# A planner's load and power times, its distance ahead of TensorE, and the last batch's end in pieces

## The chip, the core and the metric

The kernel runs on one core of a Trainium2 chip. The metric is the time of one execution on the device in microseconds. Three runs of the kernel before took 1474.4, 1475.67 and 1474.44 us; the median is 1474.44.

## What is computed

There are 16 batches of 1024 nodes with 128 features, and one adjacency matrix of 1024 x 1024 zeros and ones.

```
h   = x @ others_weight
e   = leaky_relu(pairs of u1 + u2);  att = softmax over nodes of where(adj > 0, e, -9e15)
x   = layernorm(x + att @ h + x @ self_weight)             # layer 0, a graph attention
h   = x                                                    # layer 1, a gated graph network
5 times:
    m = adj @ h
    z = sigmoid([m, m] @ w3.T + h @ u3.T + b);  r = sigmoid([m, m] @ w4.T + h @ u3.T + b)
    v = tanh([m, m] @ w5.T + (r * h) @ u5.T + b)
    h = (1 - z) * h + z * v
x   = layernorm(x + h)
```

## The kernel before

Everything is float32. The products with the adjacency matrix are made exact in two passes: `split` (L590 to 602) rounds a block to fp32r on ACT and takes the rest on DVE, and `product` (L605 to 615) sends both parts through TensorE, eight matmuls of 512 columns for a half of a batch. The gate products have float32 operands. Each batch is kept transposed (features on partitions, 1024 nodes in two halves of 512 columns) in a tile `hT`.

Batches go in pairs `q`, each with five steps `s`. For most pairs and steps, `messages` computes m of both batches together from seven products instead of eight quarters (tiles `blk_x11` to `blk_s4`, banks `ps_acc_a`, `ps_acc_c`, `gz`); for the pairs and steps in `PLAIN` each batch has its own products (`ps_acc<-adj,blk_h`). `gates` follows: a product with u3 (`pu`, L1159), a copy of its bank for z on ACT (L1162), two gate products (L1169), two tanh on ACT (L1172), r*h on DVE (L1179), two products into the bank v (L1185, L1186), tanh on ACT (`hv`, L1189) and three DVE operations that make the new h (L1196, L1203, L1210).

`leave` sends h on. As a rule the half is turned on DVE in 32x32 blocks (`turn`, L566), stored to DRAM by four DMAs (`away`, L576, X<-T) and loaded by one (`back`, L584, G<-X), which completes the transposition. Where `on_pe` says so, TensorE transposes it instead (L558) and `split` reads the bank. After the last step, `leave` loads the kept input of layer 1 (`o<-yd`, L1253), adds h (L1261), and calls `layernorm`: statistics on DVE (L527, L529), four small GpSimd instructions that make the factor and the offset (L533, L534, then L536 and L537 or, for the other sign, L539 and L540), four scales on ACT (L545), and a store (L1272). Layer 0 ends in the same `layernorm`, from `F_y` tiles that came through DRAM.

The order of the work is planned when the program is built. Every operation is added to a `Plan` with an engine, a length in nanoseconds, a rank, and the values it reads and writes. `order` plays the plan: an engine that is free takes the ready operation of the lowest rank for which tiles are free; a successor becomes ready after the length and a lag, which depends on the engine or is given with the operation. The sequence in which operations start is the program's order on every engine. On the chip each engine then takes its instructions in that order and waits for what each needs, so the planned times themselves leave no trace but the order.

The rank of a step is `10 * (b // 2) + 4.2 * s` plus an offset from the table `D` (L300). Lengths that matter here: GpSimd's part of `layernorm` 2200, the lag of `back` 2300. `IDLE` (80) and `HUM` (60) operations of two transposes of the identity each, of rank 9000, are taken by TensorE where the plan has nothing else for it; hum becomes ready only with the last pair's step 3. `o` and `y0` have two buffers each.

Of the kernel before, what the change touches and what calls it, by code (L numbers as in the profile page):

```python
# [12 lines left out]
AF = mybir.ActivationFunctionType  # L13
# [3 lines left out]
P = 128  # L17
# [8 lines left out]
LOW, HIGH = -20.0, 100.0  # L26
TINY = 1e-30
PLAIN = {(0, 0), (0, 1), (0, 2), (7, 2), (7, 3), (7, 4)}
LATER = 2.5
AHEAD = range(4, 12)  # L30
TURNED = {(0, 0), (7, 3)}
IDLE = 80
HUM = 60


class Plan:
# [36 lines left out]
    def order(self):  # L73
        ops, free = self.ops, dict(self.slots)
        users, left = [[] for _ in ops], []
        uses = {}
        for i, (_, _, _, _, deps, tiles) in enumerate(ops):
            left.append(len(deps))
            for d in deps:
                users[d].append(i)  # L80
            for t in tiles:
                uses[t] = uses.get(t, 0) + 1
        ready, busy, live = {}, {}, set()
        at = {}
        events = [(0, 0, i) for i in range(len(ops)) if not left[i]]
        heapq.heapify(events)
        started = []
        while events:
            now = events[0][0]
            while events and events[0][0] == now:  # L90
                _, what, i = heapq.heappop(events)
                engine, _, rank, _, _, tiles = ops[i]
                if what == 0:
                    heapq.heappush(ready.setdefault(engine, []), (rank, i))
                elif what == 1:
                    busy.pop(engine)
                    for t in tiles:
                        uses[t] -= 1
                        if not uses[t]:
                            free[t[0]] += 1  # L100
            more = True
            while more:
                more = False
                for engine, queue in ready.items():
                    if engine in busy:
                        continue
                    later = []
                    while queue:
# [26 lines left out]
def kernel(  # L135
# [79 lines left out]
    def exact(pools):  # L215
# [210 lines left out]
        def hum_():  # L426
            for j in range(2):
                nc.tensor.transpose(T(("ps", "hum"))[:, j * P : (j + 1) * P], ident, ident)

        def hum():  # L430
            for i in range(HUM):
                pe(2 * TR, 9000, hum_, reads=[(("m", B - 1, STEPS - 2, 1), 0)], writes=[(("ps", "hum"), 0)])

        for i in range(IDLE):
            pe(2 * TR, 9000, idle_, reads=[(("ident",), 0)], writes=[(("ps", "idle"), 0)])

# [82 lines left out]
            dve(2 * V, 1 + c / 4, t24, reads=[*y, (("tab",), c, 0)], writes=[(("tab",), c, 1)])  # L519


        def layernorm(key, g, rank, after, src, dst, write, sg=1):
            stats, mv, rstd = ("stats", *key, g), ("mv", *key, g), ("rstd", *key, g)

            def look():
# [5 lines left out]
            def power():  # L531
                mean, var, r = T(mv)[:, :, 0], T(mv)[:, :, 1], T(rstd)
                nc.gpsimd.tensor_scalar(r[:, 0, :], var, EPS, None, ALU.add)  # L533
                nc.gpsimd.tensor_tensor(r[:, 0, :], r[:, 0, :], mhalf[:, 0:4], ALU.pow)  # L534
                if sg > 0:
                    nc.gpsimd.tensor_scalar(r[:, 1, :], mean, -1.0, None, ALU.mult)  # L536
                    nc.gpsimd.tensor_tensor(r[:, 1, :], r[:, 1, :], r[:, 0, :], ALU.mult)  # L537
                else:
# [10 lines left out]
            dve(1100, rank, look, reads=[after], writes=[(stats, 0), (mv, 0)])  # L549
# [3 lines left out]
        def transposes(src, read, t, rank):  # L553


            def emit():
                for j in range(4):
                    nc.tensor.transpose(T(t)[:, j * P : (j + 1) * P], src()[:, j * P : (j + 1) * P], ident)  # L558

            pe(4 * TR, rank, emit, reads=[*read, (("ident",), 0)], writes=[(t, 0)])  # L560

        def turn(t, src, read, rank):

# [16 lines left out]
        def back(d, t, rank, also=(), then=()):  # L580
# [440 lines left out]
        def messages(q, s, k):  # L1021
# [118 lines left out]
            combine(m[one, 1], c, ALU.add)  # L1140
            return [[(m[one, 0], 0), (m[one, 1], "part")], [(m[two, 1], "part")] * 2]

        def gates(b, s, soon):
            rank = rank_of(b, s)
            hT = ("hT", b)
# [3 lines left out]
            for e in range(2):  # L1149
# [35 lines left out]
                    nc.tensor.matmul(T(pv), wm[:, 2, :], T(m), start=True, stop=False)  # L1185
                    nc.tensor.matmul(T(pv), u5h, T(r), start=False, stop=True)  # L1186

                def hv_(pv=pv, hv=hv):
                    nc.scalar.activation(T(hv), T(pv), AF.Tanh, bias=b5 if sg > 0 else nb5, scale=1.0)  # L1189

                pe(2 * F, rank + D["pv"], pv_, reads=[(m, 0), (r, 2), (("wm",), 0), (("uw",), 0)], writes=[(pv, 0)])
                act(A, rank + D["hv"], hv_, reads=[(pv, 0), (("wm",), 0)], writes=[(hv, 0)])
                dve(
                    V,
                    rank + D["h"],
                    lambda hv=hv, h=h: nc.vector.tensor_tensor(T(hv), T(hv), h(), ALU.subtract),  # L1196
                    reads=[(hv, 0), (hT, e)],
                    writes=[(hv, 1)],
                )
                dve(  # L1200
                    V,
                    rank + D["h"],
                    lambda hv=hv, z=z: nc.vector.scalar_tensor_tensor(T(hv), T(z), 1.0, T(hv), ALU.add, ALU.mult),  # L1203
                    reads=[(hv, 1), (z, 1)],
                    writes=[(hv, 2)],
                )
                dve(
                    V,
                    rank + D["h"],
                    lambda hv=hv, h=h: nc.vector.scalar_tensor_tensor(h(), T(hv), 0.5, h(), ALU.mult, ALU.add),  # L1210
                    reads=[(hv, 2)],
                    writes=[(hT, e)],
                )

        def leave(b, s):

# [2 lines left out]
            for g in range(2):  # L1219
# [18 lines left out]
                    continue  # L1238

                t = ("ps", "t", b, s, g)  # L1240
                if on_pe(b, s):
                    transposes(h, [(hT, g)], t, rank + D["tr"])
# [7 lines left out]
                sp(  # L1250
                    450,
                    rank + D["o"],
                    lambda o=o, yd=yd: nc.sync.dma_start(T(o).rearrange("p c d -> p (c d)"), T(yd)),  # L1253
                    reads=[(yd, 0), (hT, g)],
                    writes=[(o, "y")],
                )

                def last(t=t, o=o, flat=on_pe(b, s)):
                    x = T(o).rearrange("p c (a j) -> p c a j", a=4)
                    n = T(t).rearrange("p (c a j) -> p c a j", c=4, a=4) if flat else chunks(T(t))  # L1260
                    nc.vector.tensor_tensor(x, n, x, ALU.add)  # L1261

                dve(V, rank + D["o"], last, reads=[(t, 0), (o, "y")], writes=[(o, "raw")])

                def at(j, o=o):
                    return T(o)[:, j, :]

                layernorm(("o", b), g, rank + D["ln"], (o, "raw"), at, at, (o, 0), sign(b))
                sp(
                    450,  # L1270
                    rank + D["out"],
# [345 lines left out]
```

## Time and profile before

| | |
|---|---|
| median of three runs | 1474.44 us |
| the profiled execution | 1486.99 us, its span 1485.2 |
| mean granted TensorE clock | 0.995 of full speed |
| busy: TensorE, DVE, ACT, GpSimd | 1460.4, 1167.5, 900.1, 189.7 us |
| products with the adjacency (L608) | 2800 matmuls, 1.87 us for eight |
| gate products (L1159, L1169, L1185, L1186) | 0.86 us for the two passes of one |
| G<-X loads | 148 of 256 KB |
| X<-T stores | 584 of 64 KB |
| GpSimd's first instruction of a power (L533, y) | 227 to 3516 ns, median 505 |

The profile is of one execution, 12.6 us longer than the median. "Busy" of TensorE counts from a matmul's issue to its modelled end, and successive matmuls overlap, so a sum of busy times is more than the time they took; the chain of work that ended last shows what each adds. In the timeline a row has its start, its length, engine, source line, and in brackets the idle time before it and what ended that. A wait for several things is put down to the last. In the windows, each engine's busy time and number of instructions come first, then the granted clock, the share of the DMA engines, and what they moved.

### The profile page before, as it was taken

Reading aid. Unit: us, or ns where it says so; the run is one execution under the profiler, and the core shown is the slowest. Engines: PE = TensorE matmul, PEld = TensorE weight load, DVE = VectorE, ACT = ScalarE, POOL = GpSimd, SP = SyncE. Lnnn points to the kernel's source line nnn. Section 1 sums busy time; section 2 is a strip of 40 time slices with the busy share of each in tenths; the row PEclk is TensorE's granted clock in tenths of the full one; section 3 lists DMA queues with packets and bytes.
Section 4 is the critical chain, followed back from the end, with each engine's and each line's share of the span. In section 5 each row is a group of like instructions: output and inputs, shape, how many; then the busy total and the mean of one; then the engine's idle time right before and its main releaser. Section 6 shows DMA issues by size and latency. Waiting matters only on the chain.

```text
span 1485.2 us, 18097 instructions
## 1 busy us (share of the span) xinstructions
PE 1460.4 (98%) x5148; PEld 915.9 (62%) x5148; DVE 1167.5 (79%) x2761; ACT 900.1 (61%) x1800; POOL 189.7 (13%) x265
## 2 busy tenths in 40 slices
PE   9999999999999999999999999999999999999998
PEld 7666655666565666665656566565666556556666
DVE  6778688889788698988888798876888877776534
ACT  5565565666566676656756666565665666654544
POOL 0111100112111020111300121210201202000102
PEclk9999999999999999999999999999999999999999
DMA  8325724465254653445435542445433454223301
GB/s 310 135 58 167 209 68 131 125 195 162 60 145 113 196 138 87 144 146 148 116 112 139 171 135 67 133 126 152 119 96 96 138 149 113 62 71 88 107 0 45
DMA packets 210113, 184.71 MB, mean 124 GB/s; under 512 B 35071, under 2 KB 156630, under 8 KB 210006
## 3 DMA queue, kind: packets, MB, share of 16 engines
q1 hardware_dynamic: 209442, 182.64, 42.9%
q8 instruction: 42, 0.69, 0.2%
q10 hardware_dynamic: 564, 0.85, 0.2%
q14 instruction: 65, 0.53, 0.1%
HBM read 101.97 MB, written 81.44 MB: 123 GB/s over the span
## 4 chain that ended last, share of the span: by engine, by line
PE 71%; DVE 8%; DMA 7%; POOL 5%; ACT 4%; issue 2%; SPq 2%; DVEq 0%; POOLq 0%; ACTq 0%
PE ps_acc_a L608 12%; PE ps_g_r L1169 7%; PE ps_g_v L1186 7%; PE gz L1169 7%; PE ps_g_v L1185 7%; PE ps_g_r L1159 7%; PE ps_acc_c L608 7%; PE ps_acc_po L608 5%; PE ps_acc L608 4%; PE gz L608 3%; DMA G<-X 3%; SPq L576 2%; POOL rstd_y L533 2%; ACT y L545 1%; PE ps_idle L416 1%
## 5 line engine op out<-in xcount | busy, mean ns | idle before, releaser
L1196 DVE TENSOR_TENSOR hv<-hv,hT 128x512 f32<-128x512 f32 x160 | 109.8, 686 | 90.1 <-ACT hv L1189 89.4
L1169 PE MATMUL ps_g_r<-m,wm 128*128 128x512 f32 x320 | 161.3, 603 | 8.7 <-ACT gz L1162 8.7
L1186 PE MATMUL ps_g_v<-r,u5h 128*128 128x512 f32 x320 | 163.5, 592 | 0.7 <-DVE r L1179 0.7
L1185 PE MATMUL ps_g_v<-m,wm 128*128 128x512 f32 x320 | 163.6, 592 | 0.0
L1169 PE MATMUL gz<-m,wm 128*128 128x512 f32 x320 | 159.4, 595 | 0.0
L1159 PE MATMUL ps_g_r<-hT,u 128*128 128x512 f32 x320 | 154.5, 595 | 0.0
L608 PE MATMUL ps_acc_a<-tab,blk_s 128*128 128x512 f32 x544 | 147.0, 412 | 5.4 <-ACT m L1112 5.3
L608 PE MATMUL ps_acc_po<-adj,blk 128*128 128x512 f32 x512 | 140.2, 420 | 0.0
L1172 ACT ACTIVATE r<-ps_g_r,bh 128x512 f32<-128x512 f32 x160 | 109.6, 687 | 43.6 <-PE ps_g_r L1169 43.3
L1172 ACT ACTIVATE z<-gz,bh 128x512 f32<-128x512 f32 x160 | 109.0, 687 | 31.3 <-PE gz L1169 31.2
L608 PEld LDWEIGHTS ps_acc_a<-tab,blk_s 128*128 128x128 f32 x544 | 101.3, 188 | 39.8 <-ACT m L1112 8.6
L1179 DVE SCALAR_TENSOR_TENSOR r<-r,hT 128x512 f32<-128x512 f32 x160 | 108.6, 684 | 20.7 <-ACT r L1172 20.5
L533 POOL TENSOR_SCALAR rstd_y<-mv_y 128x4 f32<-128x4 f32 x32 | 30.5, 954 | 738.5 <-DVE mv_y L529 671.6
L608 PEld LDWEIGHTS ps_acc_po<-adj,blk 128*128 128x128 f32 x512 | 95.9, 188 | 35.5 <-issue 10.8
L1162 ACT COPY gz<-ps_g_r 128x512 f32<-128x512 f32 x160 | 91.3, 573 | 32.0 <-PE ps_g_r L1159 29.7
L1210 DVE SCALAR_TENSOR_TENSOR hT<-hv,hT 128x512 f32<-128x512 f32 x160 | 108.8, 680 | 1.8
L1203 DVE SCALAR_TENSOR_TENSOR hv<-z,hv 128x512 f32<-128x512 f32 x160 | 108.8, 680 | 1.0
L1186 PEld LDWEIGHTS ps_g_v<-r,u5h 128*128 128x128 f32 x320 | 60.3, 189 | 78.0 <-issue 62.9
L1169 PEld LDWEIGHTS gz<-m,wm 128*128 128x128 f32 x320 | 60.7, 191 | 72.8 <-issue 72.1
L566 DVE STREAM_TRANSPOSE T<-hT 128x512 f32<-128x512 f32 x146 | 103.0, 706 | 0.5
L608 PE MATMUL ps_acc<-adj,blk_h 128*128 128x512 f32 x384 | 102.9, 418 | 0.2 <-DVE blk_h L600 0.2
L1169 PEld LDWEIGHTS ps_g_r<-m,wm 128*128 128x128 f32 x320 | 59.7, 191 | 65.1 <-issue 37.9
(173 smaller groups left out, 2618.5 us busy)
## 6 DMA issues: line engine op xcount, KB each, us to landing
G<-X SPq DMA_DIRECT2D x148, 256.0 KB
X<-T SPq DMA_DIRECT2D x584, 64.0 KB
yd<-y SPq DMA_DIRECT2D x32, 256.0 KB
o<-yd SPq DMA_DIRECT2D x32, 256.0 KB
out_dram<-o SPq DMA_DIRECT2D x32, 256.0 KB
xt<-in_x_dram SPq DMA_DIRECT2D x15, 512.0 KB
pb<-ud SPq DMA_DIRECT2D x14, 512.0 KB
D_y<-T_y SPq DMA_DIRECT2D x112, 64.0 KB
```

Of the source, the lines that this page charges most:

```text
L566: nc.vector.transpose(T(t).rearrange("p (b c i) -> p b c i", b=4, c=4), turned(src()))
L608: nc.tensor.matmul(T(bank), T(blk)[:, k, c, :], right(c), start=(first and i == 0), stop=(last and i == len(terms) - 1), skip_group_check= ...
L1159: nc.tensor.matmul(T(pr), u3, h(), start=True, stop=True)
L1162: nc.scalar.copy(T(pz), T(pr))
L1169: nc.tensor.matmul(T(p_), wm[:, j, :], T(m), start=False, stop=True, skip_group_check=True)
L1172: nc.scalar.activation(T(t), T(p_), AF.Tanh, bias=bh[:, j : j + 1], scale=0.5 * sg)
L1179: lambda r=r, h=h: nc.vector.scalar_tensor_tensor(T(r), T(r), 1.0, h(), ALU.add, ALU.mult),
L1185: nc.tensor.matmul(T(pv), wm[:, 2, :], T(m), start=True, stop=False)
L1186: nc.tensor.matmul(T(pv), u5h, T(r), start=False, stop=True)
L1196: lambda hv=hv, h=h: nc.vector.tensor_tensor(T(hv), T(hv), h(), ALU.subtract),
L1203: lambda hv=hv, z=z: nc.vector.scalar_tensor_tensor(T(hv), T(z), 1.0, T(hv), ALU.add, ALU.mult),
L1210: lambda hv=hv, h=h: nc.vector.scalar_tensor_tensor(h(), T(hv), 0.5, h(), ALU.mult, ALU.add),
```

## The change

- The planner's lag for `back` becomes 3001 (`LATE`), GpSimd's part of `layernorm` 3001. `CARE` adds 200 where a DVE or ACT operation is followed by one of TensorE.
- Ranks: `LATER` (the last batch's shift in plain steps) 1 instead of 2.5, and nine entries of `D`.
- Step 2 of the last pair is transposed on TensorE (`TURNED`). `IDLE` is 100; hum is gone.
- In the last batch's last step the tail of `gates`, the transposes and the sum with y go in two pieces of 256 columns, and its y is loaded to buffers of `y0`, with the step's own rank, once m is there.
- In the last batch, and in half 1 of the one before, `layernorm` is short: GpSimd makes the factor alone, and DVE applies mean and factor in four operations.

```diff
-LATER = 2.5
+LATER = 1
+LATE = 3001
-TURNED = {(0, 0), (7, 3)}
-IDLE = 80
-HUM = 60
+TURNED = {(0, 0), (7, 2), (7, 3)}
+IDLE = 100
...
+    CARE = 200
...
+                                if ops[u][0] == "PE" and engine in ("DVE", "ACT"):
+                                    lag += self.CARE
...
-        D = dict(m=-0.4, pu=1.4, u=0.2, pr=0.6, pz=1.4, r=1.7, pv=0.2, z=0.3, hv=0.2, h=0.6, tr=1.2, o=4.0, ln=3.3)
-        D.update(out=4.0, l1=-9, l2=-3, l3=-3, l4=-4, l5=-5, l6=-3.5, l7=0, l8=0)
+        D = dict(m=-0.2, pu=1.4, u=0.2, pr=0.2, pz=1.4, r=1.7, pv=1.0, z=0.3, hv=0.2, h=0.8, tr=1.2, o=4.2, ln=3.3)
+        D.update(out=4.0, l1=-9, l2=-3, l3=-3, l4=-4, l5=-4, l6=-3.5, l7=0, l8=-2)
...
+                if short:
+                    if sg < 0:
+                        nc.gpsimd.tensor_scalar(r[:, 0, :], r[:, 0, :], -1.0, None, ALU.mult)
...
+            def scale_short():
+                for j in range(4):
+                    nc.vector.tensor_scalar(
+                        dst(j), src(j), T(mv)[:, j, 0:1], T(rstd)[:, 0, j : j + 1], ALU.subtract, ALU.mult
+                    )
...
-            plan.add("POOL", 2200, rank, power, reads=[(mv, 0)], writes=[(rstd, 0)])
-            act(1250, rank, scale, reads=[after, (mv, 0), (rstd, 0)], writes=[write])
+            plan.add("POOL", 2301 if short else 3001, rank, power, reads=[(mv, 0)], writes=[(rstd, 0)])
+            if short:
+                dve(900, rank, scale_short, reads=[*after, (mv, 0), (rstd, 0)], writes=[write])
+            else:
+                act(1250, rank, scale, reads=[*after, (mv, 0), (rstd, 0)], writes=[write])
...
-                lag=2300,
+                lag=LATE,
...
+        def pieces(b, s):
+
+            return 2 if b == B - 1 and s == STEPS - 1 else 1
...
+                n = pieces(b, s)
+                for i in range(n):
+                    w = slice(i * HALF // n, (i + 1) * HALF // n)
...
-                o, yd = ("o", b, g), ("yd", b, g)
+                o, yd = ("y0" if b == B - 1 else "o", b, "o", g), ("yd", b, g)
                 sp(
                     450,
-                    rank + D["o"],
+                    rank + (D["o"] if b < B - 1 else 0),
...
-                    reads=[(yd, 0), (hT, g)],
+                    reads=[(yd, 0), (hT, g) if b < B - 1 else (("m", b, s, 0), 0)],
                     writes=[(o, "y")],
+                    lag=2300,
                 )
...
+                    b == B - 1 or b == B - 2 and g,
...
-        hum()
```

More of the change, by code (lines that the diff above doesn't have):

```diff
@@ L423, in exact @@
             pe(F, -99, lambda k=k: fill_(k), reads=[(("ident",), 0)], writes=[(("gz", "fill", k), 0)])
[L426 to L432, printed above, removed]
         for i in range(IDLE):
@@ L519, in sums_of_adj, with layernorm @@
             dve(2 * V, 1 + c / 4, t24, reads=[*y, (("tab",), c, 0)], writes=[(("tab",), c, 1)])
-        def layernorm(key, g, rank, after, src, dst, write, sg=1):
+        def layernorm(key, g, rank, after, src, dst, write, sg=1, short=False):
             stats, mv, rstd = ("stats", *key, g), ("mv", *key, g), ("rstd", *key, g)
@@ L534, in power @@
                 nc.gpsimd.tensor_tensor(r[:, 0, :], r[:, 0, :], mhalf[:, 0:4], ALU.pow)
-                if sg > 0:
+                if short:
+                    if sg < 0:
+                        nc.gpsimd.tensor_scalar(r[:, 0, :], r[:, 0, :], -1.0, None, ALU.mult)
+                elif sg > 0:
                     nc.gpsimd.tensor_scalar(r[:, 1, :], mean, -1.0, None, ALU.mult)
@@ L547, in scale, with transposes @@
                     )
-            dve(1100, rank, look, reads=[after], writes=[(stats, 0), (mv, 0)])
-            plan.add("POOL", 2200, rank, power, reads=[(mv, 0)], writes=[(rstd, 0)])
-            act(1250, rank, scale, reads=[after, (mv, 0), (rstd, 0)], writes=[write])
-        def transposes(src, read, t, rank):
+            def scale_short():
[3 more added lines that the diff above has]
+                    )
+            after = after if isinstance(after, list) else [after]
+            dve(1100, rank, look, reads=after, writes=[(stats, 0), (mv, 0)])
+            plan.add("POOL", 2301 if short else 3001, rank, power, reads=[(mv, 0)], writes=[(rstd, 0)])
[3 more added lines that the diff above has]
+                act(1250, rank, scale, reads=[*after, (mv, 0), (rstd, 0)], writes=[write])
+        def transposes(src, read, t, rank, cs=range(4), part=0):
             def emit():
-                for j in range(4):
+                for j in cs:
                     nc.tensor.transpose(T(t)[:, j * P : (j + 1) * P], src()[:, j * P : (j + 1) * P], ident)
-            pe(4 * TR, rank, emit, reads=[*read, (("ident",), 0)], writes=[(t, 0)])
+            pe(len(cs) * TR, rank, emit, reads=[*read, (("ident",), 0)], writes=[(t, part)])
         def turn(t, src, read, rank):
@@ L1186, in pv_ @@
                     nc.tensor.matmul(T(pv), u5h, T(r), start=False, stop=True)
-                def hv_(pv=pv, hv=hv):
-                    nc.scalar.activation(T(hv), T(pv), AF.Tanh, bias=b5 if sg > 0 else nb5, scale=1.0)
                 pe(2 * F, rank + D["pv"], pv_, reads=[(m, 0), (r, 2), (("wm",), 0), (("uw",), 0)], writes=[(pv, 0)])
[L1192 to L1213, printed above, removed]
+                n = pieces(b, s)
@@ new lines, in gates, with hv_, less_, times_ @@
+                for i in range(n):
+                    w = slice(i * HALF // n, (i + 1) * HALF // n)
+                    def hv_(pv=pv, hv=hv, w=w):
+                        nc.scalar.activation(T(hv)[:, w], T(pv)[:, w], AF.Tanh, bias=b5 if sg > 0 else nb5, scale=1.0)
+                    def less_(hv=hv, h=h, w=w):
+                        nc.vector.tensor_tensor(T(hv)[:, w], T(hv)[:, w], h()[:, w], ALU.subtract)
+                    def times_(hv=hv, z=z, w=w):
+                        nc.vector.scalar_tensor_tensor(T(hv)[:, w], T(z)[:, w], 1.0, T(hv)[:, w], ALU.add, ALU.mult)
+                    def h_(hv=hv, h=h, w=w):
+                        nc.vector.scalar_tensor_tensor(h()[:, w], T(hv)[:, w], 0.5, h()[:, w], ALU.mult, ALU.add)
+                    length = V if n == 1 else V / n + 40
+                    act(
+                        A if n == 1 else 400,
+                        rank + D["hv"],
+                        hv_,
+                        reads=[(pv, 0), (("wm",), 0)],
+                        writes=[(hv, 0, i)],
+                    )
+                    dve(length, rank + D["h"], less_, reads=[(hv, 0, i), (hT, e)], writes=[(hv, 1, i)])
+                    dve(length, rank + D["h"], times_, reads=[(hv, 1, i), (z, 1)], writes=[(hv, 2, i)])
+                    dve(length, rank + D["h"], h_, reads=[(hv, 2, i)], writes=[(hT, e) if n == 1 else (hT, e, i)])
@@ L1240, in leave @@
                 t = ("ps", "t", b, s, g)
+                n = pieces(b, s)
+                done = [(hT, g)] if n == 1 else [(hT, g, i) for i in range(n)]
                 if on_pe(b, s):
-                    transposes(h, [(hT, g)], t, rank + D["tr"])
+                    for i in range(n):
+                        transposes(h, [done[i]], t, rank + D["tr"], range(4 * i // n, 4 * (i + 1) // n), i)
                 else:
@@ L1247, in leave, with last @@
                     back(d, t, rank + D["o"])
-                o, yd = ("o", b, g), ("yd", b, g)
+                o, yd = ("y0" if b == B - 1 else "o", b, "o", g), ("yd", b, g)
                 sp(
                     450,
-                    rank + D["o"],
+                    rank + (D["o"] if b < B - 1 else 0),
                     lambda o=o, yd=yd: nc.sync.dma_start(T(o).rearrange("p c d -> p (c d)"), T(yd)),
-                    reads=[(yd, 0), (hT, g)],
+                    reads=[(yd, 0), (hT, g) if b < B - 1 else (("m", b, s, 0), 0)],
                     writes=[(o, "y")],
+                    lag=2300,
                 )
[L1258 to L1263, printed above, removed]
+                for i in range(n):
+                    def last(i=i, t=t, o=o, flat=on_pe(b, s)):
+                        cs = slice(4 * i // n, 4 * (i + 1) // n)
+                        x = T(o)[:, cs, :].rearrange("p c (a j) -> p c a j", a=4)
+                        v = T(t).rearrange("p (c a j) -> p c a j", c=4, a=4) if flat else chunks(T(t))
+                        nc.vector.tensor_tensor(x, v[:, cs], x, ALU.add)
+                    dve(V / n, rank + D["o"], last, reads=[(t, i), (o, "y")], writes=[(o, "raw", i)])
                 def at(j, o=o):
                     return T(o)[:, j, :]
-                layernorm(("o", b), g, rank + D["ln"], (o, "raw"), at, at, (o, 0), sign(b))
+                layernorm(
+                    ("o", b),
+                    g,
+                    rank + D["ln"],
+                    [(o, "raw", i) for i in range(n)],
+                    at,
+                    at,
+                    (o, 0),
+                    sign(b),
+                    b == B - 1 or b == B - 2 and g,
+                )
                 sp(
```

## The prediction

> **What bounds the kernel now.** I read the page's busy shares first, then the waits of TensorE, then the timeline around the longest waits, the clock in short windows, and the timeline of the end.
>
> ```profile
> PE 1460.4 (98%) x5148; PEld 915.9 (62%) x5148; DVE 1167.5 (79%) x2761; ACT 900.1 (61%) x1800; POOL 189.7 (13%) x265
> ```
>
> TensorE is the bound: 98% busy, DVE next at 79%. But not all of that is work of the reference, as the groups of TensorE show (busy, mean ns, idle before):
>
> ```profile
> L416 PE MATMUL ps_idle<-ident 128*128 128x128 f32 x160 | 21.4, 280 | 0.0
> L428 PE MATMUL ps_hum<-ident 128*128 128x128 f32 x120 | 13.6, 273 | 0.0
> ```
>
> These are filler. In the chain of waits four transposes take 0.44 us, so one costs 0.109 us of TensorE. The waits of TensorE (total, times, longest):
>
> ```profile
> PE ps_g_r L1169 <- ACT gz L1162: 8.7, 7, 2.7
> PE ps_acc_a L608 <- ACT m L1112: 5.3, 5, 2.2
> PE gz L608 <- ACT gz L1112: 2.7, 1, 2.7
> PE gz_fill L420 <- POOL ones L386: 1.3, 1, 1.3
> PE ps_g_v L1186 <- DVE r L1179: 0.7, 1, 0.7
> ...
> ```
>
> Without the start's 1.3 they add up to 18.8 us. ACT copies are named, but they are late for what stands ahead of them in ACT's order. One wait, in the timeline:
>
> ```profile
> 474.49 3.52 POOL L533 TENSOR_SCALAR rstd_y<-mv_y 128x4 f32<-128x4 f32 x1 [32.00 <-DVE mv_y L529]
> ...
> 479.76 1.65 ACT L545 ACTIVATE y<-F_y,rstd_y 128x128 f32<-128x128 f32 x4 [3.43 <-POOL rstd_y L537]
> 481.31 0.58 ACT L1112 COPY gz<-ps_acc_a 128x512 f32<-128x512 f32 x1
> ...
> 481.94 3.45 PE L608 MATMUL gz<-adj,blk_x 128*128 128x512 f32 x8 [2.67 <-ACT gz L1112]
> ```
>
> GpSimd took 3.52 us for an instruction whose median is 0.5 and 5.2 us (474.49 to 479.72) for the four that the planner counts as 2.2. ACT stood 3.43 us at the scale behind it, and the copy that TensorE needed stood behind that. I traced the others back in the same way. GpSimd: 2.67, 2.22, 1.92, 0.69 (7.5 us). Loads `G<-X` of 2.8 to 5.3 us where the planner counts 2.3, or the stores before them: 2.69, 2.00, 1.56, 1.19 (7.4). The remaining 3.9 are pieces of 0.2 to 0.7. ACT waits 50.4 us for G loads and 55.6 for GpSimd's powers in all, most of it unseen by TensorE. The windows around the waits (PE, PEld, DVE, ACT, POOL busy, then clock, DMA share, GB/s):
>
> ```profile
> 375.00:380.00 5.00, 2.78 (x11) 1.71 (x10) 4.45 (x12) 2.37 (x6) 2.60 (x1) 1.00 0.01 2
> 480.00:485.00 5.00, 3.06 (x8) 2.44 (x9) 4.26 (x13) 3.33 (x8) 2.65 (x4) 0.66 0.45 133
> 1190.00:1195.00 5.00, 4.79 (x11) 3.06 (x12) 2.59 (x4) 2.12 (x5) 0.00 (x0) 0.66 0.74 224
> ```
>
> A mean of 0.66 over 5 us is 3.4 us at half clock. It happens four times (also 188 to 191 and 1024 to 1028), after waits of 2.00, 2.67, 2.69 and 1.92, and not after 2.22. Half clock for 3.4 us costs 1.7, together 6.8. Last, the end:
>
> ```profile
> 1464.11 1.02 PE L1186 MATMUL ps_g_v<-r,u5h 128*128 128x512 f32 x2
> ...
> 1472.26 0.32 SPq L1253 DMA_DIRECT2D o<-yd  x1
> ...
> 1474.92 0.69 DVE L1261 TENSOR_TENSOR o<-ps_t,o 128x512 f32<-128x512 f32 x1 [4.58 <-DMA o<-yd]
> ...
> 1478.94 1.65 ACT L545 ACTIVATE o<-o,rstd_o 128x128 f32<-128x128 f32 x4 [4.53 <-POOL rstd_o L537]
> ```
>
> The last gate's product streams out at 1465.0 (two passes of 0.43); the span ends 20.2 us later. In it the last residual load starts at 1472.26, because a buffer of o had to come free, and DVE stands 4.58 us for it.
>
> **The change, part by part**, against the profiled execution (span 1485.2, time 1487.0).
>
> *TensorE's order up to the last gate's product.* I lay the two built orders end to end with the chain's durations (product of eight 1.87, 512-column fp32 pass pair 0.86, transpose 0.109). Before: 1429.8 us; after: 1437.5. The 7.6 are: filler 200 instead of 154 transposes ahead of that point (+5.0); sixteen transposes for step 2 of the last pair (+1.75); one gate that now stands ahead of the last product (+0.86). 106 fillers lie in the first 24 us in both, where the loads set the pace. The new ones stand mostly at 48 to 53 us (36 instead of 6) and 72 to 76 (20 instead of 8). Before waited only 0.28 and 0.48 there, and GpSimd's four take 2.6 and 3.0 there; so I charge this filler in full. What hum did after the last product is hidden by the 20 us of the end; dropping it is nothing.
>
> *Longer times for loads (2.3 to 3.0) and powers (2.2 to 3.0), 0.2 more from ACT and DVE to TensorE, new ranks.* No work is added; ACT, DVE, SP and TensorE are reordered. For each G load I added up the TensorE time between the product that makes its h and the first TensorE instruction that needs ACT's cast or anything behind it on ACT. Before, 12 of 120 loads have under 16 us, the least 12.9; after, 1 of 116, the least 14.6. The two whose loads cost 2.00 and 1.56 had 15.5 to 16.3 and get 16.4 to 19. For the first layernorm, 7 of 32 are under 18 us before, 3 after; the case above (19.1) leaves the twelve least, all under 24. So each class gains some 1 to 3 us where it is tightest, as much as the waits. I leave 1.5 of the loads' 7.4, 1.0 of GpSimd's 7.5 and 2.0 of the small 3.9.
>
> *The last stage.* Two batches alone must hide each other. With step 2 turned on TensorE, sixteen X stores, four G loads and four DVE turns go, and so does the gap that 14 fillers held at 1401 to 1402.5. But the order now sets transposes closer behind the product that makes h: 3.9 to 4.3 us at five of ten places, against 5.0 to 5.3 before. In the trace h is ready 3.4 us after the product where DVE is free (1448.9 to 1452.3) and 4.3 where it does a layernorm between (1454.2 to 1458.5). I add 2.0 us of new waits, between 0 and 7. Waits together: 18.8 to 6.5, -12.3.
>
> *The clock.* The Trainium skill ("TensorE: Matmul & The Clock Gate", What's actually happening) has the half clock come only after at least one idle window of about 3.4 us. By that rule none of these waits could drop it, there would be nothing to win, and the sum would be 5.1 worse. The rows contradict it: waits of 1.9 to 2.7 did, so the measurement decides. With waits mostly under 1.5 I leave one of four: -5.1.
>
> *The end.* The y load of the last batch goes to y0's buffers and is issued once m of the last step is there, well over 10 us ahead of need. On SP the loads of batch 14 stand behind it, and those need a later h, so nobody waits: the 4.58 go. Two GpSimd steps go (0.24 + 0.20 and gaps: 0.6), ACT's four scales (1.65) become four on DVE; a DVE tensor_scalar of 128x128 took 0.216, so 0.9. Against that, halves cost DVE more: a 128x262 copy took 0.37 on ACT where 512 took 0.57, and scaled alike six halves of 0.45 stand for three of 0.68 (+0.65). Also batch 14's second scale (0.9) and both halves' statistics (1.25 each) now stand in one DVE row. From the product: tanh to 0.8, three steps in halves to 3.6, sum of half 0 to 4.5, scale of batch 14 to 5.4, statistics 6.6, sum and statistics of half 1 to 8.8, power 10.3, scale 11.2, store 4.6 (as 1480.6 to 1485.2): 15.8 instead of 20.2, -4.4; 0 to -7 if DVE's order binds or hides more.
>
> **Sum:** 7.6 - 12.3 - 5.1 - 4.4 = -14.2, so 1472.8 profiled. The runs shown have a median of 1474.44, 12.6 below the profiled one. The profiled span is 1429.8 order + 4.5 start + 20.2 end + 30.7 waits, clock and refills. If the 12.6 all come out of the last term, it is 18.1 in the runs (59%), the 17.4 saved become 10.3, and the change is -7.1: 1467.3. If the profile shows the runs' waits truly, 1460.2. I take the middle, **1463.8**, with 1458 to 1469 its own range.
>
> **Rivals.**
> - *All waits go.* 2 us of waits left, no half clock: 7.6 - 16.8 - 6.8 - 4.4 = -20.4; 1454.0, or 1463.7 by the 59%; about 1456. For it: the margins grew by as much as the waits. Against: loads of 5.3 us where the 16 DMA engines are 90 to 100% busy, as around 160 and 170 us.
> - *Traded.* Other places with thin margins start to wait (loads collide elsewhere, filler delays); half of the saving is lost: -14.2 + 8.7 = -5.5 or less, 1469 to 1474. For it: filler is charged for certain, waits saved only by likelihood.
> - *Slower.* The last stage has lost its cover: all filler is spent by about 390 us, and the transposes follow h so closely that TensorE stands at each of the ten places. At 1.5 us each and two spells of half clock that is 18.4; with the 59%: 7.6 - 4.4 - 0.59 x 21.1 + 18.4 = +9.2, 1483. It decides from about 0.6 us a place. Against: h needs 3.4 to 4.3, so only five places are short, by less than 0.7.
> - *It doesn't do what it says:* the built order shows the margins, the halves and the early loads; only their worth is open.
>
> **Chances:** forecast 0.60 and all-go 0.15, both faster; traded 0.16, half faster and half no change; slower 0.09, of it 0.07 beyond 0.2% and 0.02 within. A measurement of this kernel can tell about 0.2% (3 us) from no change. Faster 0.83, same 0.10, slower 0.07. Range: 1453 takes in most of all-go, 1472 most of traded; left out are the slower case, traded's end and a little below, under 0.2.
>
> **What would show it.** Right: ACT's waits for G and powers well under 50.4 and 55.6; TensorE's waits about 6; the clock at half once or never; the o load landed before its sum; 15 to 16 us from the last gate's product to the end; `ps_idle` x200 with TensorE busy at 48 to 53 us. Wrong: waits of TensorE for `ps_t<-hT` beyond 1360 us, `G<-X` still above 4 us with a copy behind it, or waits above 12 us in all.

## The result, and the profile after

| | before | after |
|---|---|---|
| median of 13 runs each | 1473.81 us | 1467.45 us |
| lowest to highest | 1470.7 to 1477.89 | 1465.32 to 1470.91 |
| ratio after/before | | 0.9959, 95% interval 0.9948 to 0.9969 |
| profiled execution, its span | 1486.99, 1485.2 | 1466.94, 1465.1 |
| ACT's waits for G loads, for powers | 56.4, 55.6 | 32.9, 3.0 |
| GpSimd's instructions of a layernorm over 1.85 us | 15 | 1 |

The change makes the kernel 0.4% faster, some 6 us. The forecast of 1463.8 had the sign and most of the mechanism, and was 3.6 us too low; its reading "59%" gave 1467.3. The profiled execution fell by 20.0 us, three times as much as the runs. The page of after, the busy line:

```profile
PE 1444.8 (99%) x5084; PEld 907.3 (62%) x5084; DVE 1170.5 (80%) x2777; ACT 896.5 (61%) x1790; POOL 157.0 (11%) x260
```

TensorE is still the bound. GpSimd fell from 189.7 to 157.0, far more than the five instructions that were dropped. Four of the lines behind the table's sums of ACT's waits (total, times, longest), two of before and two of after:

```profile
ACT blk_x L596 <- DMA G<-X: 50.4, 29, 5.1
ACT y L545 <- POOL rstd_y L537: 19.5, 10, 3.4
...
ACT blk_x L603 <- DMA G<-X: 27.2, 20, 3.7
ACT y L542 <- POOL rstd_y L534: 1.6, 1, 1.6
```

What TensorE waited for in after:

```profile
PE ps_t L565 <- DVE hT L1214: 3.3, 2, 2.3
PE ps_g_v L1197 <- DVE r L1190: 2.7, 2, 2.1
PE gz_fill L423 <- POOL ones L389: 1.3, 1, 1.3
PE ps_acc L615 <- ACT blk_h L603: 0.8, 1, 0.8
PE ps_g_r L1180 <- ACT gz L1173: 0.5, 1, 0.5
PE ps_acc L615 <- DVE blk_h L607: 0.4, 1, 0.4
```

Without the start these are 7.7 us; the 2.3 are the last transposes behind the last gate's product, where they cost nothing more than the end itself. So 5.4 stand ahead of that product, where before had 18.8. All the waits for a copy of m are gone, and 8.7 for gz became 0.5. The longest ahead of that product is at 504.47, and the clock behind it (busy of PE, PEld, DVE, ACT, POOL, then clock, DMA share, GB/s):

```profile
505.00:510.00 5.00, 5.00 (x9) 2.09 (x8) 4.96 (x16) 2.72 (x6) 2.19 (x4) 0.66 0.36 99
```

A clock of 0.66 over 5 us is 3.4 us at half clock. That is the one spell ahead of the end. The end of after in the timeline:

```profile
1449.47 1.02 PE L1197 MATMUL ps_g_v<-r,u5h 128*128 128x512 f32 x2
1450.53 0.84 ACT L1205 ACTIVATE hv<-ps_g_v,b 128x256 f32<-128x256 f32 x2 [0.22 <-PE ps_g_v L1197]
...
1456.10 0.72 DVE L1281 TENSOR_TENSOR y_o<-ps_t,y_o 128x256 f32<-128x256 f32 x2
...
1459.55 1.11 DVE L548 TENSOR_SCALAR y_o<-y_o,mv_o,rstd_o 128x128 f32<-128x128 f32 x4 [0.68 <-POOL rstd_o L528]
```

The product has streamed out at 1450.3 and the span ends at 1465.1: 14.8 us, before 20.2. The sum with y (1456.10) has no wait of 4.58 in front of it any more; the two loads of y were issued at 1374.8 and 1375.4, 78 us ahead of the first sum's start.

### The profile page after: what moved, and what is told of

It reads as the page before. It is cut to its first block, busy times and chain, and to the rows that moved or that the text cites. A ratio compares the mean times of both kernels' runs of the same rounds, so it can differ in the third digit from the quotient of the medians.

```text
span 1465.1 us, 17965 instructions
## 1 busy us (share of the span) xinstructions
PE 1444.8 (99%) x5084; PEld 907.3 (62%) x5084; DVE 1170.5 (80%) x2777; ACT 896.5 (61%) x1790; POOL 157.0 (11%) x260
## 5 line engine op out<-in xcount | busy, mean ns | idle before, releaser
L1208 DVE TENSOR_TENSOR hv<-hv,hT 128x512 f32<-128x512 f32 (+1 forms) x162 | 109.8, 679 | 56.5 <-ACT hv L1205 56.0
L615 PEld LDWEIGHTS ps_acc_po<-adj,blk 128*128 128x128 f32 x512 | 96.0, 188 | 35.3 <-issue 10.3
L1214 DVE SCALAR_TENSOR_TENSOR hT<-hv,hT 128x512 f32<-128x512 f32 (+1 forms) x162 | 108.0, 670 | 1.7
L1211 DVE SCALAR_TENSOR_TENSOR hv<-z,hv 128x512 f32<-128x512 f32 (+1 forms) x162 | 108.1, 670 | 1.5 <-ACT z L1183 0.4
L573 DVE STREAM_TRANSPOSE T<-hT 128x512 f32<-128x512 f32 x142 | 99.0, 700 | 0.2
L615 PE MATMUL ps_acc<-adj,blk_h 128*128 128x512 f32 x384 | 97.6, 407 | 1.2 <-ACT blk_h L603 0.8
L603 ACT CAST blk_s<-G 128x512 fp32r<-128x512 f32 x136 | 82.9, 617 | 22.0 <-DVE G L1061 19.1
L607 DVE TENSOR_TENSOR blk_s<-G,blk_s 128x512 fp32r<-128x512 f32 x136 | 90.7, 678 | 6.8 <-ACT blk_s L603 6.2
```

Of the source, the lines that this page charges most:

```text
L573: nc.vector.transpose(T(t).rearrange("p (b c i) -> p b c i", b=4, c=4), turned(src()))
L615: nc.tensor.matmul(T(bank), T(blk)[:, k, c, :], right(c), start=(first and i == 0), stop=(last and i == len(terms) - 1), skip_group_check= ...
L1208: nc.vector.tensor_tensor(T(hv)[:, w], T(hv)[:, w], h()[:, w], ALU.subtract)
L1211: nc.vector.scalar_tensor_tensor(T(hv)[:, w], T(z)[:, w], 1.0, T(hv)[:, w], ALU.add, ALU.mult)
L1214: nc.vector.scalar_tensor_tensor(h()[:, w], T(hv)[:, w], 0.5, h()[:, w], ALU.mult, ALU.add)
```

## The experiments

To compare kernels I cut each profiled span as the prediction did: the built order laid end to end up to the last gate's product, 4.5 us of start, the end from that product on, and a *third term* that is left over (waits, half clock, and small gaps that the list of waits doesn't show). Where a gate stands behind the last product (before, and the new end alone), the end contains it.

| kernel | median | ratio to before, interval | order | third term | end | span |
|---|---|---|---|---|---|---|
| before, as profiled | 1473.81 | 1 | 1429.8 | 30.7 | 20.2 | 1485.2 |
| after | 1467.45 | 0.9959 (0.9948 to 0.9969) | 1437.5 | 8.3 | 14.8 | 1465.1 |
| new end only | 1470.62 | 0.9966 (0.9952 to 0.9979) | 1430.0 | 15.5 | 18.8 | 1468.8 |
| after with the old end | 1473.46 | 0.9984 (0.9972 to 0.9996) | 1437.5 | 8.2 | 20.5 | 1470.7 |
| after, IDLE 53 | 1466.18 | 0.9939 (0.9925 to 0.9953) | 1427.2 | 17.8 | 14.9 | 1464.4 |
| after, filler's bank held | 1465.97 | 0.9929 (0.9915 to 0.9942) | 1437.7 | 7.8 | 15.6 | 1465.6 |
| after with the old times | 1488.26 | 1.0082 (1.0063 to 1.0101) | 1437.9 | 30.6 | 14.6 | 1487.6 |
| before with the new times | 1471.52 | 0.9971 (0.9959 to 0.9984) | 1432.9 | 15.8 | 17.8 | 1471.0 |
| after, halves whole | 1467.53 | 0.9950 (0.9934 to 0.9965) | 1437.5 | 8.3 | 14.8 | 1465.1 |
| after, old load time | 1477.12 | 1.0023 (1.0014 to 1.0033) | 1437.5 | 20.2 | 14.9 | 1477.1 |
| after, old power time | 1474.19 | 0.9997 (0.9988 to 1.0006) | 1437.5 | 15.8 | 16.0 | 1473.8 |
| after, no CARE | 1468.88 | 0.9960 (0.9947 to 0.9974) | 1437.9 | 13.4 | 15.1 | 1470.9 |
| before, new end and new times | 1466.25 | 0.9951 (0.9936 to 0.9965) | 1432.9 | 10.2 | 16.3 | 1463.9 |

A median is of that kernel's own runs, and before's own median differed from group to group (1473.81 beside after, 1475.68 beside the first four kernels, 1474.6 and 1474.54 beside the others), so the ratios compare kernels across groups. Two of the profiles lie above their medians, "old load time" by 2.0 and "no CARE" by 3.9 us, so their third terms are high by about as much. None of these kernels leaves out a part of what the reference computes.

**The new end on the kernel before.** The end's code is that of after; all constants, ranks, times and filler are those of before.

```diff
-LATER = 1
-LATE = 3001
+LATER = 2.5
+LATE = 2300
...
+IDLE = 80
+HUM = 60
...
-    CARE = 200
+    CARE = 0
```

> The kernel before with the new end alone (pieces, short layernorm, early load of y to y0's buffers); times, ranks, turned steps, idle and hum as before. First theory, that the end is a separate gain of some 5.4 us (in the profiles 20.2 us from the last gate's product to the end before, 14.8 after) and the new times, ranks and filler together nearly cancel: -5.4, about 0.9963 of before. Rival, that the gain comes from the waits of TensorE and the end is worth little in the runs: within 0.1% of before.

The ratio is 0.9966, 5.0 us less than before's 1475.68 beside it. In the profile the stretch from the last gate's product to the end lost only 1.4 of its 20.2. The work in it is as short as in after: from 1449.97, where the product has streamed out, to the end of the last scale at 1460.32 it takes 10.4 us (10.3 in after, 15.6 in before). What comes behind the last scale takes 8.4 us instead of after's 4.5. Three lines show why: the last scale in the timeline, the filler in the chain that ended last, and what SyncE (SP in the rows) waited for in its closing lines:

```profile
1459.20 1.12 DVE L557 TENSOR_SCALAR y_o<-y_o,mv_o,rstd_o 128x128 f32<-128x128 f32 x4 [0.24 <-POOLq L1606]
...
1454.48 10.92 PE ps_hum L431 x100
...
SPq L1651 <- PEq L1606: 3.8, 1, 3.8
```

`HUM` is 60 here, and its 120 transposes run on to 1465.4; SyncE, which closes the program, waits 3.8 us for TensorE's queue. So the new end needs hum to go as well, which this kernel leaves in.

The waits of TensorE ahead of the end are the old planner's:

```profile
PE ps_g_r L1189 <- ACT gz L1182: 6.8, 9, 1.6
...
PE ps_acc_a L624 <- ACT m L1128: 1.2, 2, 0.8
```

Together 11.1 us without the start, none over 1.6, and no spell of half clock. This execution lay at its kernel's median (1470.61). So the old ranks and times can run with a third term of 15.5, against 30.7 in before's profile. Up to 359 us every engine has the same order in both kernels, and there the two executions differ too: the gate's product at 188 us waits 0.94 us here and keeps its clock, where before's profile has 2.00 and a spell of half clock.

**The old end on the kernel after**, the reverse.

```diff
-            return 2 if b == B - 1 and s == STEPS - 1 else 1
+            return 1
...
-                    b == B - 1 or b == B - 2 and g,
+                    False,
...
-                    rank + (D["o"] if b < B - 1 else 0),
+                    rank + D["o"],
```

> The changed kernel with the end of before (whole halves, four scales on ACT, late load to o's buffers); TensorE's order up to the last gate's product has the same length. First theory: the 5.4 us come back, so about 0.9996 of before, no gain left. Rival, that waits carry the gain: stays at 0.996.

The end is 20.5 instead of 14.8, and the time 6.0 us over after's by the medians, 4.3 by the ratios. With no hum in either kernel, this is the cleaner measure of the end. What is left, the new order alone, is worth 0.16%, some 2.4 us: a third term of 8.2, bought with 7.7 us of order.

**Less filler at the head.** `IDLE` 53 takes 94 transposes out, 10.3 us of order.

```diff
-IDLE = 100
+IDLE = 53
```

> The changed kernel with 53 instead of 100 filler operations, so that filler stands in the first 24 us alone; TensorE's order up to the last product is 10.3 us shorter. First theory, that filler is charged in full where the kernel before waited little: 4 to 8 us less than the changed kernel, 0.991 to 0.993 of before, waits between 24 and 390 us up by a few us. Rival, that filler only fills gaps which are there anyway: 0.995 to 0.997, waits up by about 10 us in that stretch, perhaps with spells of half clock.

Neither: 1.3 us faster than after by the medians, up to 3 by the ratios. The order is 10.3 shorter and the third term 9.5 longer. TensorE's waits in this kernel:

```profile
PE ps_t_u L683 <- ACT u L668: 3.6, 1, 3.6
PE ps_acc L615 <- DVE blk_h L607: 3.0, 3, 2.0
...
PE ps_ahead L455 <- DVE rz L824: 1.3, 1, 1.3
```

In the timeline they lie at 9 to 60 and at 160 to 180 us (after's filler ends by 377), and 6.8 us of half clock at 160 to 170. So this filler costs a tenth to a third of its length, if the order that the planner built around it is not worth as much by chance (next experiment): the rest fills time that the loads and ACT take in any case.

**The filler's bank.** When the last filler is planned, its PSUM bank goes back to the pool and the planner has one more. One more filler, ready only at the end, keeps it.

```diff
+        pe(2 * TR, 9000, idle_, reads=[(("m", B - 1, STEPS - 1, 1), 0)], writes=[(("ps", "idle"), 0)])
         for i in range(2 * NC):
             look_at(i)
```

> The changed kernel with one more filler operation that becomes ready only at the last step, so that the filler's tile holds one of the six PSUM banks to the end, as idle's and hum's did before; in the changed kernel it is free from some 390 us on. First theory, that times and ranks made the margins: within 0.1% of the changed kernel, 0.996. Rival, that the free bank gives TensorE its distance: waits of TensorE back above 12 us, 0.998 to 1.0 of before.

The bank doesn't matter for the gain: third term 7.8, no half clock ahead of the end. The kernel is even a little faster than after (its ratio's interval lies below that of after's 13 runs, and just overlaps that of the runs below), with an order that one operation reshuffled. So 0.1 to 0.3% between two kernels may be no more than chance in the built order.

**After once more.**

> The changed kernel itself, as the measure for the other three on the same chip: 0.996 of before by both theories; its waits of TensorE (7.7 us in the first profile) show how much one execution differs from the next.

Median 1467.48, ratio 0.9951 (0.9935 to 0.9968), the wait of the gate's product at 504 us and the one spell of half clock at the same place. For after, one profile speaks for the kernel.

**The old times with the new ranks.**

```diff
-LATE = 3001
+LATE = 2300
-    CARE = 200
+    CARE = 0
-            plan.add("POOL", 2301 if short else 3001, ...
+            plan.add("POOL", 1500 if short else 2200, ...
```

> The changed kernel with the planner's old times (loads 2300, powers 2200, no 200 more towards TensorE); ranks, turned steps, filler and end as changed; TensorE's order is as long (1437.9 us up to the last product). In it 8 loads have under 16 us to hide in, against 1 in the changed kernel and 12 before. First theory, that the times make the distance: waits of TensorE back by 4 to 5 us, 0.999 of before. Rival, that the ranks and the turned step do: as the changed kernel, 0.996.

I had the sign and missed the size: 21 us slower than after, slower than before too. TensorE's waits:

```profile
PE ps_g_r L1180 <- ACT gz L1173: 5.9, 6, 3.7
PE ps_t L565 <- DVE hT L1214: 5.0, 3, 3.5
PE ps_t_u L683 <- ACT u L668: 4.1, 2, 2.1
PE ps_acc_a L615 <- ACT m L1119: 3.3, 1, 3.3
PE gz L615 <- ACT gz L1119: 2.0, 3, 1.1
```

Four spells of half clock, at 165 to 170, 380, 560 and 915. ACT waits 75.6 us for G loads. With the old times the new ranks do harm.

**The new times with the old ranks**: before, with 3001 for loads and powers and the 200 ns ahead of TensorE, and nothing else.

```diff
-                lag=2300,
+                lag=3001,
-            plan.add("POOL", 2200, ...
+            plan.add("POOL", 3001, ...
+                                if ops[u][0] == "PE" and engine in ("DVE", "ACT"):
+                                    lag += 200
```

> The kernel before with the planner's new times alone; ranks, turned steps, filler operations, hum and end as before. TensorE's order up to the last product is 3.1 us longer (more of the filler falls before it). First theory: waits 5 us less, so 2 us faster, 0.9985 of before. Rival, that the times alone do nothing for the margins (11 loads still under 16 us) and only add filler: 1.001 to 1.002.

0.9971: 4.3 us, twice what I gave it. ACT's waits fall to 43.7 for loads and 25.8 for powers. The end, with before's code, is 17.8 instead of 20.2; its last sum waits 2.77 us for its load and not 4.58.

**Halves not cut** in the last step of the last batch.

```diff
-            return 2 if b == B - 1 and s == STEPS - 1 else 1
+            return 1
```

> The changed kernel with the last batch's last step in whole halves of 512 columns instead of pieces; short layernorm and early load stay. First theory, from the rows (six pieces against three wholes on DVE): the stretch from the last gate's product to the end gets about 0.6 us shorter than 14.8. Rival, that the pieces overlap ACT, DVE and TensorE: it gets 0.3 to 1 us longer. Both are within the noise of the time; the trace tells.

No difference: 1467.53, and an end of 14.8 us as well. Here TensorE's last transposes wait 4.07 us instead of 2.31, but DVE does other rows of the end meanwhile; it is DVE's work, not the way of one half, that sets the end. The pieces are worth nothing; the early load and the short layernorm, with hum gone, are the end's gain. No run has one of these alone.

**Which of the times?** Three kernels, each after with one time set back.

```diff
-LATE = 3001
+LATE = 2300
```

> The kernel after with the planner's lag for the loads back at 2300; CARE and GpSimd's 3001 stay. All three times back cost 21 us (1488.3 against 1467.5). Theory, the loads carry it: their ACT waits for G grew most there (32.9 to 75.6 us), so this alone costs 8 to 15 us: 1475 to 1482, TensorE's waits 12 to 18, two or more spells of half clock. Rival, no time carries it alone and only their sum makes margins thin: under 4 us, 1464 to 1471. Rival, GpSimd's time carries it: within 2 us of 1467.5.

```diff
-            plan.add("POOL", 2301 if short else 3001, ...
+            plan.add("POOL", 1500 if short else 2200, ...
```

> The kernel after with GpSimd's part of a layernorm back at 2200 (1500 in the short form); the loads' 3001 and CARE stay. Theory, the loads carry the 21 us: this costs 2 to 4 us, 1469 to 1472, ACT's waits for powers from 3 to about 25 us. Rival, GpSimd's time carries it: 8 to 15 us, 1475 to 1482. Rival, only the sum: under 4 us as well, and then the other two tell.

```diff
-    CARE = 200
+    CARE = 0
```

> The kernel after without the 200 ns ahead of TensorE; the loads' and GpSimd's 3001 stay. Theory, the loads carry the 21 us: 1 to 3 us, 1468 to 1471, a few more waits of 0.2 to 0.7 us for gz and r. Rival, the distance is what keeps TensorE free of ACT and DVE everywhere: 8 us or more, 1475 and up, waits behind ps_g_r, gz and ps_t in the list.

Against after's ratio (0.9955 between its two groups of runs): the loads' time 0.68%, 10.0 us; GpSimd's 0.42%, 6.2 us, more than the 2 to 4 that I gave it; CARE 0.05%, 0.7 us, not told from nothing. Together 16.9 of the 18.7 that all three cost by the ratios: they add, and the loads carry most. How a load's time reaches TensorE is seen in the first of them:

```profile
732.82 0.62 ACT L603 CAST blk_x<-G 128x512 fp32r<-128x512 f32 x1 [5.19 <-DMA G<-X]
733.35 0.59 ACT L1121 ACTIVATE m<-ps_acc_a 128x512 f32<-128x512 f32 x1
...
733.99 2.50 PE L615 MATMUL ps_acc_a<-tab,blk_x 128*128 128x512 f32 x5 [2.87 <-ACT m L1121]
```

The planner thought the load would have landed and put its cast ahead of the copy of m. ACT stands 5.19 us at the cast, and TensorE, which waits for the copy, 2.87; half clock follows. SyncE issued the load at 730.02, so 2.4 us of ACT's wait passed before it was issued and 2.8 after. After puts the copies first: ACT's waits for loads are 82.9 us here and 32.9 there. My measure of thin margins fails this test, though: by it this kernel has one load under 16 us, as after has, and it is 10 us slower. It counts TensorE's time between a half and its use, and leaves out when DVE turns the half and when the load can start.

How GpSimd's time reaches TensorE is shown less well. With it set back, ACT's waits for powers rise from 3.0 to 19.9 us, but only two of TensorE's waits, 1.01 and 0.91 us, stand behind such a scale. Its longest two (4.08 and 1.87, at 178.10 and 180.76), with 6.8 us of half clock, stand behind ACT's waits for loads, as the order there changed with the rest. So the 6.2 us are what this kernel lost, and not all of it by powers that came late.

```profile
177.43 0.62 ACT L603 CAST blk_h<-G 128x512 fp32r<-128x512 f32 x1 [2.60 <-DMA G<-X]
178.10 0.79 PE L615 MATMUL ps_acc<-adj,blk_h 128*128 128x512 f32 x1 [4.08 <-ACT blk_h L603]
```

**The new end and the new times on before**, with the old ranks, `IDLE`, hum and `TURNED`.

> The kernel before with the new end and the three new times; ranks, IDLE 80, hum and TURNED as before. The end alone was worth 5.0 us, the times alone 4.3. Theory, they add, as one shortens the stretch behind the last product and the other the waits ahead of it: -9.3 of about 1475, so 1465 to 1467, no slower than the kernel after, and the new ranks, the turned step and the longer filler are worth nothing. Rival, both gains are in good part the same relief of a stall, or a reshuffled order eats one: 1469 to 1472.

0.9951: as fast as after. The two parts add up to 9.3 and give 7.2, equal within their intervals. So the new ranks (seven entries of `D` differ in the diff, not nine, and `LATER`), the turned step and the change of filler bring together nothing that these runs can tell, once times and end are new. Hum stays in this kernel and sets its end too, as SyncE's last wait shows; without hum it might be faster than after. No run tried that.

```profile
SPq L1651 <- PEq L1606: 2.0, 1, 2.0
```

## Why the prediction was right in sign, and where its size failed

**The order's +7.6 and the filler.** The order was as built, and so were its counts; the new filler stands at 52 to 60 and 76 to 81 us, some 4 us later than said. But "I charge this filler in full" was wrong as a cost: most of it stands in for time that would else be spent waiting. The sum hides this, since the waits that it replaces are on the other side.

**The waits.** Said: 6.5 ahead of the last product; found: 5.4. ACT's waits for powers went from 55.6 to 3.0, for loads from 56.4 to 32.9 (the prediction's 50.4 left out the 6.0 for `blk_h`), and the waits named for a copy with them. The direction is shown by the kernels with single times set back, and the head-of-line mechanism by the rows of the one with the old load time; for powers it is argued. The last stage: said 2.0 new, found 1.5 (0.58 at 1370.86, 0.96 at 1378.10), so the rival "slower", which needed 0.6 at each of ten places, had no ground. What the turned step itself was worth was not run.

**The clock.** Said: one spell left; found: one, behind a wait of 2.09 us. The rows held here too, and not the idle window of some 3.4 us that the Trainium skill ("TensorE: Matmul & The Clock Gate", What's actually happening) has the half clock come after. But the -5.1 compares two profiled executions; see the mis-sized step.

**The end.** Said 15.8; found 14.8. The mis-sized term is the DVE operation of 256 columns: 0.36 (0.72 for two) where I scaled 0.45; ten of them lie in the row. And "dropping it is nothing" holds of hum only beside before's end of 20 us: the kernel with the new end alone stood 3.8 us for it.

**The mis-sized step: "I take the middle."** The profile of before was one execution 12.6 us over its median, and I split the difference between "all of the 17.4 is saved in the runs" and "59% of it". At the medians (span 1472.0, 1.8 below the time) before's third term is 1472.0 - 1429.8 - 4.5 - 20.2 = 17.5, if order and end are as profiled; after's is 8.8. So waits and clock saved 8.7, where the two readings have 10.3 and 17.4: 7.7 - 8.7 - 5.4 = -6.4, which is the measured difference by construction. The kernel with the new end alone, profiled at its own median, bears the lower level out: a third term of 15.5, 11.1 of it waits, and no half clock.

The record settles the clock's part. It lists the mean granted clock of every execution. A spell of 3.4 us takes 0.0012 off the mean, and before's profiled execution, with four, has 0.995. Of the 91 executions of before beside the experiments none is that low: 59 have 0.999 or 1.0, which leaves room for one spell at most, and another 24 have 0.998, two at most. So 5 us or more of the 12.6 by which the profiled execution was too long are half clock, and of the 5.1 that I took for the clock a usual run could give 1.7 at most. For the waits the same is argued only: no profile of before at its median exists here.

I had held the low reading to be a bound; it was near the measure. That it comes so close, 1467.3, is partly luck: it saves 1.6 too much in waits and clock and 1.0 too little at the end, and starts from a median 0.6 too high. Of the rivals' sums one is off: the middle of all-go's 1454.0 and 1463.7 is 1458.9, not 1456.

**A cause that I had wrong.** I took GpSimd's 3.52 us for 128x4 elements as a slow instruction that comes by chance, to be planned for. The trace of before shows more. In its 15 instructions over 1.85 us, GpSimd works beside a row on DVE with hardly a break, such as this one in the timeline (start, length, engine):

```profile
721.29 4.54 POOL L536 TENSOR_SCALAR rstd_o<-mv_o 128x4 f32<-128x4 f32 x1
721.43 0.67 DVE L792 SCALAR_TENSOR_TENSOR junk<-adj,pb 128x512 f32<-128x512 f32 x1
...
724.46 0.67 DVE L1210 SCALAR_TENSOR_TENSOR hT<-hv,hT 128x512 f32<-128x512 f32 x1
725.06 0.67 DVE L792 SCALAR_TENSOR_TENSOR junk<-adj,pb 128x512 f32<-128x512 f32 x1
...
725.67 0.69 DVE L566 STREAM_TRANSPOSE T<-hT 128x512 f32<-128x512 f32 x1
```

But for reads of an accumulator (0.07 each), every DVE operation from 721.43 on takes two tensors from SBUF; the GpSimd instruction ends at 725.83, when DVE has gone over to one that reads one. The case that the prediction quotes is of the same kind: 474.49 to 478.01, and the transpose starts at 477.83. At least ten of the fifteen end within 0.2 us of such a change or of a gap on DVE. The Trainium skill ("GPSIMD Engine Reference", Specifications) has the two engines share their SBUF interfaces, with contention from DVE instructions that read two SBUF inputs, which fits these rows. It is read from traces, not tried by an experiment. What the runs do show: such instructions number 15 in before and 9 in the kernel with the new end alone, 3 with the new times on before, 2 with the old times on the new ranks, 1 in after. So a new order goes with fewer of them, whichever part brings it; that it breaks the rows up is argued. It isn't the whole of the time: the slowest kernel of all has 2.

**What stays open.** Why the new ranks cost so much with the old times (1.0082 against 0.9966 with the old ranks, 17 us) is known only as far as the list of waits goes. Why before's profiled execution had three spells more than most is open too, and so is how much of the end the early load, the short layernorm and the drop of hum each carry.

## What to carry to other kernels

Where a planner sets the order in which an engine takes its work, a time that is too short for a load or a small GpSimd chain costs at another place than that load: the queue behind it stands, and the engine that is late is the one that needs the next entry. Plan such times for their bad cases, and set ranks again only after that: the new ranks, harmless with the new times, cost 17 us with the old. When an end is shortened, look again at filler that it used to hide. And set a profiled execution beside the median first: a sum of waits from one that is 0.85% over its kernel's median is no measure of what a change can save.

## What the runs showed of the hardware

- Half clock for 3.4 us came behind single waits of TensorE of 2.09 (after), 2.53 and 2.87 us (old load time), and in the last kernel (new end and new times on before) with two of 1.44 and 1.02 that ended at 162.65 and 164.17. It did not come in kernels whose longest waits ahead of the end were 1.6 and 1.3, nor behind single ones of 1.87 (halves whole), 2.16 (before with the new times) and 2.22 (before). So the length of one wait does not decide it in these traces.
- In before, GpSimd took up to 4.54 us for 512 elements beside rows of two-input DVE operations; an instruction of the same line took 0.24 us at 372.78.
- At the end of the kernel two DVE operations of 256 columns took 0.72 to 0.76 us together in after, and one of 512 took 0.66 to 0.68 in the kernel with whole halves: cutting a half in two was nearly free on DVE.
- The new end alone closed 3.8 us late behind 120 transposes that nothing read: SyncE waited for TensorE's queue at the program's end.
